# A post-norm decoder layer on one core: projections, feed-forward inputs and spline chunks dealt out in a new order

## The chip, the cores and the metric

The kernel runs on one core of a Trainium2 chip. The core has five engines that run their own instruction streams and meet at semaphores: TensorE (PE in the profile, with PEld for its weight loads), VectorE (DVE), ScalarE (ACT), GpSimd (POOL) and SyncE (SP). DMA transfers are issued from the streams of SP, ACT and POOL. TensorE writes its results to PSUM, from where VectorE and ScalarE copy them out.

The metric is the device time of one execution in microseconds. The kernel before took 601.08 us in the median of 3 runs (600.80, 601.08 and 601.48).

## The reference

The input is x, 8 sequences (batches) of 256 tokens with 512 features, and a context of the same shape, all in fp32. One layer is computed, with a layer norm after each of its three parts:

```
x = layernorm(x + attention(x))                   # 16 heads of 32, q, k, v through low-rank maps, softmax, Wo
x = layernorm(x + x * r)                          # r: per head r[t] = decay * r[t-1] + ctx[t] * ctx[t]
x = layernorm(x + down @ (silu(gate @ x) * up @ x))
```

The three feed-forward weights (512 x 2048, twice, and 2048 x 512) are not given: each is a cubic spline through about 8,000 control points, sampled at every weight. The kernel uses that a spline is a cubic between its knots, so it never builds the dense weights: per tile of 128 inner features it needs 64 numbers for each token (samples of x near the knots and moments of x over the pieces between them), and 64 x 128 spline samples as weights. These samples are made on the chip from control points ("taps").

## The kernel before, in words

**Tiling.** The 2048 tokens are four groups g of 512 tokens (GT, NG), and a group is two batches (bb). Heads are taken in quads of four. The attention loop has 4 groups x 2 batches x 4 quads = 32 steps, s0 to s31 (`steps`, L634). All engine calls go through `Ordered` (L299), which keeps program order on each engine, so every row of the profile carries line L308 and is known by its tile names.

**A step.** Step s first issues the score matmuls of step s + 1 (`scores`: 8 matmuls into four PSUM tiles sc of ps_big). Then it works on the exponentials of its own four heads: `transposed` (4 transposes a head into a PSUM tile tr_e), `evicted` (copy to eT: heads 0 and 2 by VectorE, 1 and 3 by ScalarE), in the order tr0, tr1, tr2, `fill(2)`, tr3, `fill(6)`; in group 3 the last is `fill(2)`. Between them stand the row maxima (nmax, VectorE) and exponentials (ScalarE) of step s + 1. Last comes `weighted`, 8 matmuls into av. An av tile serves two quads and is freed by a multiply with the reciprocal sums (rec) in the step after.

**PSUM.** Two pools of four tiles: ps_big holds sc, and ps_mm holds everything else of the loop: tr_e, the units' results, av, tr_r, tr_rec, tr_x2, ps_mom. A tile of ps_mm comes free when its eviction has read it.

**Units and fill.** `units` is a list of generators, each a piece of TensorE work cut into steps of one call: a projection (`project`: 4 matmuls of 128 x 512 for one of 4 rows of q, k or v of the next group, 12 units a group), an output (`output`: 4 matmuls with Wo for 128 tokens; its eviction adds x and starts a chain of norms), and the inputs of a feed-forward block (`inputs`: 8 pieces: four times 4 transposes of x2 with an eviction to x2T, then four times the matmuls of the moments ps_mom). `fill(n)` (L354) takes n pieces from the head of the list. After every second piece it runs `slot()`, which advances every chain of norms by a stage, and `some_taps()` (L442), which adds 0.62 to a counter and, for each whole, makes one chunk of spline samples: a load on SP into one of two tiles, and multiplies and adds on POOL into wg, wu or wd. Sixteen chunks are for gate and up, forty for down. Before each group's end the loop at L771 takes all remaining projections of the next group, and `load_x` puts the load of x of the group after next on SP; xT_g has one buffer.

**Chains.** A norm is `norm_plain` (a square with sum on ScalarE, then va and rs on POOL, then x on VectorE) and later `norm_wide` (its rc on VectorE waits for rs of POOL). Between them come the transposes tr_r of the recurrence r and the multiply h on VectorE that frees tr_r. `recur` loads and squares the context on POOL and scans it on VectorE.

**Inputs.** `inputs(b)` needs x2 of block b. Its eviction goes to a DRAM scratch (xd, md), and `windows` and `moments` read it back on SP into xg, of which two tiles exist. Inputs 0 and 1 are units of group 3.

**Feed-forward (L984 on).** For each block b of 512 tokens: 16 gate and up matmul pairs (`gate_up`), a gather of inter on SP, 64 thin matmuls y (`exact`), sums (`into_sums`, which end in DMAs fin<-sum from POOL) and `finish`, which adds the last matmuls into y. inputs(b + 1) is a unit of blocks 1 and 2; reads that were put off are issued after that block's gate_up.

Of the kernel before, what the change touches and what calls it, by code (L numbers as in the profile page):

```python
# [10 lines left out]
F32 = mybir.dt.float32  # L11
# [6 lines left out]
P = 128  # L18
# [297 lines left out]
def decoder_kernel(ctx: ExitStack, tc: tile.TileContext, x, xT, ctxT, wq, wkT, wvT, woT, wdownT, wup, decay, up_taps, down_taps, mom_f, sum_f, out, plan):  # L316
# [37 lines left out]
    def fill(n):  # L354

        for i in range(n):
            if units:
                next(units[0][1])
                units[0][2] -= 1
                if not units[0][2]:  # L360
                    units.pop(0)
            if i % 2:
                slot()
                some_taps()

# [52 lines left out]
    folded, qkvs, rs, sums, xs, yTs = {}, {}, {}, {}, {}, {}  # L418
    dram = ctx.enter_context(tc.tile_pool(name="dram", bufs=2, space=bass.MemoryType.DRAM))

    def taps():

        todo = [(up_taps, s, (wg, wu)) for s in range(INTER // 2 // CH)]
        todo += [(down_taps, s, (wd,)) for s in range(wd.shape[1] // CH)]
        loaded = []
        for at in range(len(todo) + 1):
            if at < len(todo):
                src, s, ws = todo[at]
                c = att.tile([P, 3, 4, CH], F32, tag="taps", name="taps", bufs=2)
                nc.sync.dma_start(out=c[:, : len(ws) + 1], in_=src[s])  # L430
                loaded.append(c)
            if at:
                _, s, ws = todo[at - 1]
                c = loaded.pop(0)
                for j, w in enumerate(ws):
                    c4 = c[:, j + 1]
                    nc.gpsimd.tensor_tensor(c4, c4, c[:, 0], ALU.mult)
                    nc.gpsimd.tensor_tensor(c4[:, 0:2, :], c4[:, 0:2, :], c4[:, 2:4, :], ALU.add)
                    nc.gpsimd.tensor_tensor(w[:, s * CH : (s + 1) * CH], c4[:, 0, :], c4[:, 1, :], ALU.add)
            yield  # L440

    def some_taps():  # L442
        made[0] += 0.62
        while made[0] >= 1:
            made[0] -= 1
            next(weights, None)

    weights, made = taps(), [0]
# [5 lines left out]
    def load_x(g):  # L454
        xT_g = early.tile([P, DC, GT], F32, tag="xT", name="xT_g")
        nc.sync.dma_start(out=xT_g, in_=xT[:, g * GT : (g + 1) * GT].rearrange("(c p) t -> p c t", p=P))
        return xT_g
# [10 lines left out]
    def project(g, name, m, xT_g):  # L468

        ps = ps_mm.tile([P, GT], F32, tag="mm", name=f"ps_{name}")  # L470
        for c in range(DC):
            if name == "v":
                lhsT, rhs = xT_g[:, c, m * P : (m + 1) * P], folded[name][:, c, :]
            else:
                lhsT, rhs = folded[name][:, c, m * P : (m + 1) * P], xT_g[:, c, :]
            nc.tensor.matmul(ps, lhsT=lhsT, rhs=rhs, start=(c == 0), stop=(c == DC - 1))
            if c < DC - 1:
                yield
        evict_qkv(g, name, m, ps)
        yield  # L480

    def projections(g, xT_g):
        qkvs[g] = group_tiles(g)
        return [[name, project(g, name, m, xT_g), DC] for name in "qkv" for m in range(DC)]
# [125 lines left out]
    w_v = early.tile([P, DC, D], F32, name="w_v")  # L610
    w_o = last.tile([P, DC, D], F32, name="w_o")
    folded.update(q=w_q, k=w_k, v=w_v)
    xT_g = early.tile([P, DC, GT], F32, tag="xT", name="xT_g")
# [42 lines left out]
    for name in "qv":  # L656
        for m in range(DC):
            for _ in project(0, name, m, xT_g):
                pass
    xT_g = load_x(1)  # L660
# [39 lines left out]
    def inputs(b):  # L700
# [5 lines left out]
        xg = pool.tile([P, NTILE // 2, GT], F32, tag="xg", name="xg", bufs=2)  # L706
        xgs[b] = xg
# [10 lines left out]
        if b > 1:  # L718
            reads.append(lambda: windows(xd, xt, xg))
        else:  # L720
            windows(xd, xt, xg)
        mo = ffn["mom"].tile([P, ND, GT], F32, tag="fin", name="mom")
        ps = {}
        for c in range(DC):
# [13 lines left out]
            if c == DC - 1:  # L738
# [4 lines left out]
                if b > 1:  # L743
                    reads.append(lambda: moments(md, xg))
                else:
                    moments(md, xg)
# [5 lines left out]
    for s, (g, bb, quad) in enumerate(steps):  # L752
        n = g * 2 + bb
        if quad == 0 and bb == 0:
            if g + 1 < NG:
                units += projections(g + 1, xT_g)
            else:
                first.close()
                open_inputs()
                units += [["i", inputs(0), 2 * DC], ["i", inputs(1), 2 * DC]]  # L760
        if quad == 0 and n:
            load_rows(n - 1)
            o = [["o", output(n - 1, qc), DC] for qc in range(2)]
            if bb and g + 1 < NG:
                units[1:1] = o[:1]
                units.append(o[1])
            else:
                units[1:1] = o
            chains.append(recur(n))
        more = s + 1 < len(steps)  # L770
        if more and steps[s + 1][0] != g:  # L771
            while any(u[0] != "o" for u in units):
                fill(4)
            if g + 2 < NG:
                xT_g = load_x(g + 2)
        if more:
            sc = scores(s + 1)
# [41 lines left out]
        fill(2)  # L819
# [7 lines left out]
        fill(6 if g + 1 < NG else 2)  # L827
# [18 lines left out]
    for _ in weights:  # L846
        pass
# [136 lines left out]
    for b in range(NG):  # L984
        if 0 < b < NG - 1:
            units.append(["i", inputs(b + 1), 2 * DC])
            fill(DC)
        for j in range(NTILE // 2):
# [5 lines left out]
            if b and j == 2:  # L994
                fill(DC)
# [75 lines left out]
```

## Time and profile before

| | |
|---|---|
| median of 3 runs | 601.08 us |
| span of the profiled execution | 599.9 us |
| time outside the span, against the median | 1.2 us |
| step 4 to 5, scores end to scores end (102.99 to 114.06) | 11.07 us |
| attention steps s24 to s31 (329.90 to 399.58) | 69.68 us, PE busy 63.46 |
| feed-forward (400 to 600) | PE busy 188.23 of 200 us |
| POOL busy, 60 to 146 us | 59.41 us |

In a row of the timeline the columns are the start, the length, the engine, the line and the operation with out<-in and its shape; a bracket gives the idle time of the engine just before it and what ended it. "x12" means that twelve equal instructions in a row are drawn together. A projection, output or moments row counts a matmul in two to four records, so `ps_k x4` is two pieces of a unit and takes about 1.8 us. A step is best measured from the end of its sc row to the end of the next.

### The profile page before, as it was taken

What the parts mean: (1) busy time and instruction counts of PE and PEld (TensorE: products, weight loads), DVE (VectorE), ACT (ScalarE), POOL (GpSimd) and SP (SyncE); (2) the same over time, 40 slices, a digit from 0 to 9 for tenths busy, and PEclk for the clock granted to TensorE, in tenths of its full rate; (3) what the DMA queues carried; (4) which work ended last, traced back from release to release, by engine and by line L of the source; (5) the groups of instructions that cost most, each with busy time, mean ns of one, the idle gap of its engine ahead of it and who ended that gap; (6) DMA issues with size and microseconds to landing.
All of it is one profiled execution on the core that took longest, in us unless ns stands there. A gap on an engine that the chain in (4) does not pass through costs nothing.

```text
span 599.9 us, 9721 instructions
## 1 busy us (share of the span) xinstructions
PE 573.7 (96%) x3327; PEld 289.1 (48%) x3327; DVE 335.5 (56%) x741; ACT 274.3 (46%) x820; POOL 229.3 (38%) x513
## 2 busy tenths in 40 slices
PE   8999999988899999999999899999999999999993
PEld 3544545545455555555555556444344434433432
DVE  0203645558686575786664877776826505714615
ACT  0114644655655645654554677564315314504412
POOL 0000496686554535365440212200361262242253
PEclk9999999999999999999999999999999999999997
DMA  8104134335334115323210564659219987985931
GB/s 289 71 0 153 34 122 144 105 98 174 94 85 158 50 59 176 107 89 124 70 54 2 174 155 109 170 154 213 47 72 248 195 232 179 226 216 135 216 128 70
DMA packets 41696, 77.95 MB, mean 130 GB/s; under 512 B 5952, under 2 KB 10448, under 8 KB 41648
## 3 DMA queue, kind: packets, MB, share of 16 engines
q1 hardware_dynamic: 34576, 62.75, 39.8%
q0 software_dynamic: 6064, 13.41, 6.8%
q10 hardware_dynamic: 1008, 1.18, 0.7%
q8 instruction: 26, 0.43, 0.3%
q14 instruction: 22, 0.18, 0.1%
HBM read 45.22 MB, written 11.12 MB: 94 GB/s over the span
## 4 chain that ended last, share of the span: by engine, by line
PE 77%; DVE 7%; DMA 6%; POOL 5%; issue 2%; ACT 2%; POOLq 0%; SPq 0%; DVEq 0%; ACTq 0%
PE y L308 10%; PE ps_q L308 8%; PE ps_k L308 8%; PE ps_v L308 8%; PE ps_o L308 6%; PE tr_e L308 6%; PE pg L308 5%; PE ps_s L308 5%; PE av L308 5%; PE pu L308 5%; PE sc L308 4%; POOL taps L308 3%; PE ps_mom L308 2%; DMA fin<-sum 2%; DVE nmax L308 2%
## 5 line engine op out<-in xcount | busy, mean ns | idle before, releaser
L308 ACT ACTIVATE e<-sc,nmax 128x256 f32<-128x256 f32 x256 | 120.0, 479 | 76.2 <-DVE nmax L308 76.0
L308 DVE TENSOR_REDUCE nmax<-sc 128x2 f32<-128x512 f32 x128 | 85.2, 682 | 72.0 <-PE sc L308 67.0
L308 POOL TENSOR_TENSOR taps<-taps 128x256 f32<-128x256 f32 (+1 forms) x144 | 87.9, 610 | 33.8 <-DMA taps<-in_down_taps 25.8
L308 PE MATMUL tr_e<-ident,e 128*128 128x128 f32 x512 | 68.0, 276 | 0.8 <-DVE h L308 0.7
L308 PEld LDWEIGHTS tr_e<-ident,e 128*128 128x128 f32 x512 | 57.3, 140 | 22.7 <-issue 19.1
L308 PE MATMUL y<-inter,wd 32*128 32x512 f32 x512 | 63.0, 598 | 0.0
L308 PE MATMUL ps_o<-w_o,yT 128*128 128x512 f32 x128 | 60.0, 600 | 0.3 <-ACT eT L308 0.3
L308 PE MATMUL ps_v<-w_v,xT_g 128*128 128x512 f32 x128 | 58.6, 598 | 0.9 <-DVE eT L308 0.9
L308 PE MATMUL ps_k<-xT_g,w_k 128*128 128x512 f32 x128 | 58.7, 600 | 0.5 <-DMA xT_g<-in_xT 0.5
L308 PE MATMUL ps_q<-xT_g,w_q 128*128 128x512 f32 x128 | 58.2, 596 | 0.9 <-DVE eT L308 0.9
L308 ACT ACTIVATION_READ_ACCUMULATOR e<-sc,nmax 128x1 f32 x256 | 53.1, 207 | 0.0
L308 DVE TENSOR_TENSOR inter<-pu,sg 128x512 f32<-128x512 f32 x64 | 41.2, 687 | 18.3 <-PE pu L308 9.4
L308 POOL TENSOR_TENSOR rs<-va,neghalf 128x1 f32<-128x1 f32 x48 | 28.9, 602 | 49.6 <-DVE va L308 46.9
L308 ACT ACTIVATE sg<-pg 128x512 f32<-128x512 f32 x64 | 37.3, 597 | 18.4 <-PE pg L308 18.4
L308 POOL TENSOR_SCALAR va<-ss 128x1 f32<-128x1 f32 x32 | 6.5, 203 | 100.7 <-ACT x L308 51.1
L308 DVE COPY eT<-tr_e 128x512 f32<-128x512 f32 x64 | 43.8, 684 | 0.8 <-PE tr_e L308 0.7
L308 PEld LDWEIGHTS y<-inter,wd 32*128 32x128 f32 x512 | 26.7, 184 | 32.7 <-issue 27.0
L308 PE MATMUL av<-eT,v_g 128*32 128x256 f32 x512 | 36.7, 385 | 5.0 <-ACT eT L308 2.7
L308 POOL TENSOR_TENSOR r<-r 128x1024 f32<-128x1024 f32 x8 | 15.2, 1895 | 66.0 <-DMA r<-in_ctxT 65.9
L308 ACT COPY eT<-tr_e 128x512 f32<-128x512 f32 x64 | 37.3, 583 | 2.4 <-PE tr_e L308 2.4
L308 PE MATMUL sc<-k_g,q_g 32*128 32x256 f32 x512 | 37.4, 401 | 0.2 <-ACT e L308 0.2
L308 PEld LDWEIGHTS ps_v<-w_v,xT_g 128*128 128x128 f32 x128 | 23.1, 190 | 26.0 <-issue 24.3
(106 smaller groups left out, 739.8 us busy)
## 6 DMA issues: line engine op xcount, KB each, us to landing
nat<-inter SPq DMA_DIRECT2D x64, 256.0 KB
taps<-in_down_taps SPq DMA_DIRECT2D x40, 256.0 KB
taps<-in_up_taps SPq DMA_DIRECT2D x16, 384.0 KB
xg<-xd SPq DMA_DIRECT2D x8, 616.0 KB
r<-in_ctxT SPq DMA_DIRECT2D x8, 512.0 KB
x_t<-in_x SPq DMA_DIRECT2D x16, 256.0 KB
fin<-sum POOLq DMA_DIRECT2D x16, 256.0 KB, 5.3
out<-h SPq DMA_DIRECT2D x16, 256.0 KB
```

What stands on the lines that cost most here:

```text
L308: return lambda *a, **k: self.tc.keep_in_program_order(f(*a, **k))
```

## The change

- `fill` takes a number of slots. Every step calls `fill(2, 1)` and then `fill(FILLS[g][quad % 2], 3)`: 7 and 6 pieces a step in turn in group 0, 8 and 8 in group 1, 7 and 8 in group 2, 6 and 6 in group 3, always with four slots. Before, it was 8, 8, 8 and 4 pieces, with as many slots as half of that.
- Projections follow ORDER: the first batch's v before the later q and k, and the second batch's v (v2, v3) last. The latter are projected within the group that uses them. `require` takes pieces from the list, without slots, until a named unit is done: q and k of a quad before its scores, v before `weighted`, and all but the last two units of group 3 before its start.
- Outputs and inputs are put at other places of the list. inputs(2) is a unit of group 3, no longer of block 1, and its reads are issued in block 0. xg is allocated at the first read (`gathered`).
- `some_taps` adds 0.5 for the first sixteen chunks and 0.66 after; chunks left at the start of group 3 are made there.
- `load_x` of a group is issued when v3 of the group before is projected, on ScalarE's queue for groups 2 and 3.
- xT_g and w_v move to the pool att, the taps tiles to early.
- After the loop the remaining units are taken with `fill(2)`.

```diff
--- before.py
+++ after.py
@@ -351,17 +351,23 @@
             if next(c, c) is c:
                 chains.remove(c)
 
-    def fill(n):
-
+    def fill(n, slots=None):
+
+        slots = n // 2 if slots is None else slots
         for i in range(n):
             if units:
                 next(units[0][1])
                 units[0][2] -= 1
                 if not units[0][2]:
                     units.pop(0)
-            if i % 2:
+            if (i + 1) * slots // n > i * slots // n:
                 slot()
                 some_taps()
+
+    def require(g, *names):
+
+        while any(u[0] == (g, name) for u in units for name in names):
+            fill(1, 0)
 
     def norm_plain(h, s, o, other=None):
 
@@ -415,7 +421,9 @@
 
 
 
-    folded, qkvs, rs, sums, xs, yTs = {}, {}, {}, {}, {}, {}
+    FILLS = (5, 4), (6, 6), (5, 6), (4, 4)
+    ORDER = [(name, int(m)) for name, m in ("q0", "k0", "v0", "v1", "q1", "k1", "q2", "k2", "q3", "k3", "v2", "v3")]
+    folded, qkvs, rs, sums, xs, yTs, xTs = {}, {}, {}, {}, {}, {}, {}
     dram = ctx.enter_context(tc.tile_pool(name="dram", bufs=2, space=bass.MemoryType.DRAM))
 
     def taps():
@@ -426,7 +434,7 @@
         for at in range(len(todo) + 1):
             if at < len(todo):
                 src, s, ws = todo[at]
-                c = att.tile([P, 3, 4, CH], F32, tag="taps", name="taps", bufs=2)
+                c = early.tile([P, 3, 4, CH], F32, tag="taps", name="taps", bufs=2)
                 nc.sync.dma_start(out=c[:, : len(ws) + 1], in_=src[s])
                 loaded.append(c)
             if at:
@@ -440,20 +448,21 @@
             yield
 
     def some_taps():
-        made[0] += 0.62
+        made[0] += 0.5 if made[1] < INTER // 2 // CH else 0.66
         while made[0] >= 1:
             made[0] -= 1
+            made[1] += 1
             next(weights, None)
 
-    weights, made = taps(), [0]
+    weights, made = taps(), [0, 0]
 
     def group_tiles(g):
         pool, tag = (att, "odd") if g % 2 else (early, "even")
         return [pool.tile([P, DC, GT], F32, tag=f"{n}_{tag}", name=f"{n}_g") for n in "qkv"]
 
     def load_x(g):
-        xT_g = early.tile([P, DC, GT], F32, tag="xT", name="xT_g")
-        nc.sync.dma_start(out=xT_g, in_=xT[:, g * GT : (g + 1) * GT].rearrange("(c p) t -> p c t", p=P))
+        xT_g = att.tile([P, DC, GT], F32, tag="xT", name="xT_g")
+        (nc.scalar if g > 1 else nc.sync).dma_start(out=xT_g, in_=xT[:, g * GT : (g + 1) * GT].rearrange("(c p) t -> p c t", p=P))
         return xT_g
 
     def evict_qkv(g, name, m, ps):
@@ -465,8 +474,9 @@
         else:
             nc.scalar.copy(o, ps)
 
-    def project(g, name, m, xT_g):
-
+    def project(g, name, m):
+
+        xT_g = xTs[g]
         ps = ps_mm.tile([P, GT], F32, tag="mm", name=f"ps_{name}")
         for c in range(DC):
             if name == "v":
@@ -477,11 +487,13 @@
             if c < DC - 1:
                 yield
         evict_qkv(g, name, m, ps)
-        yield
-
-    def projections(g, xT_g):
+        if g and (name, m) == ORDER[-1] and g + 1 < NG:
+            xTs[g + 1] = load_x(g + 1)
+        yield
+
+    def projections(g):
         qkvs[g] = group_tiles(g)
-        return [[name, project(g, name, m, xT_g), DC] for name in "qkv" for m in range(DC)]
+        return [[(g, f"{name}{m}"), project(g, name, m), DC] for name, m in ORDER]
 
     def recur(n):
 
@@ -607,10 +619,10 @@
     bd_vo = early.tile([P, P], F32, name="bd_vo")
     w_q = early.tile([P, DC, D], F32, name="w_q")
     w_k = early.tile([P, DC, D], F32, name="w_k")
-    w_v = early.tile([P, DC, D], F32, name="w_v")
+    w_v = att.tile([P, DC, D], F32, name="w_v")
     w_o = last.tile([P, DC, D], F32, name="w_o")
     folded.update(q=w_q, k=w_k, v=w_v)
-    xT_g = early.tile([P, DC, GT], F32, tag="xT", name="xT_g")
+    xT_g = xTs[0] = att.tile([P, DC, GT], F32, tag="xT", name="xT_g")
     for c in range(DC):
         nc.sync.dma_start(out=w_k[:, c, :], in_=wkT[c * P : (c + 1) * P, :])
         nc.scalar.dma_start(out=xT_g[:, c, :], in_=xT[c * P : (c + 1) * P, 0:GT])
@@ -655,9 +667,9 @@
         (nc.vector.tensor_copy if m % 2 else nc.scalar.copy)(w_q[:, m, :], ps)
     for name in "qv":
         for m in range(DC):
-            for _ in project(0, name, m, xT_g):
+            for _ in project(0, name, m):
                 pass
-    xT_g = load_x(1)
+    xTs[1] = load_x(1)
     chains.append(recur(0))
     sc = scores(0)
     es = [exponentials(0, j, sc[j]) for j in range(4)]
@@ -703,8 +715,12 @@
         xt = pool.tile([P, DC, GT], F32, tag="x2T", name="x2T")
         xd = dram.tile([4 * SPAN, GT], F32, tag="xd", name="xd")
         md = dram.tile([1, 20 * NTILE, GT], F32, tag="md", name="md")
-        xg = pool.tile([P, NTILE // 2, GT], F32, tag="xg", name="xg", bufs=2)
-        xgs[b] = xg
+
+        def gathered():
+            if b not in xgs:
+                xgs[b] = pool.tile([P, NTILE // 2, GT], F32, tag="xg", name="xg", bufs=2)
+            return xgs[b]
+
         for c in range(DC):
             tr = ps_mm.tile([P, GT], F32, tag="mm", name="tr_x2")
             for t in range(TC):
@@ -716,9 +732,9 @@
                 nc.sync.dma_start(out=xd[row : row + 4 * c - 3 : 4, :], in_=xt[:c, c, :])
             yield
         if b > 1:
-            reads.append(lambda: windows(xd, xt, xg))
+            reads.append(lambda: windows(xd, xt, gathered()))
         else:
-            windows(xd, xt, xg)
+            windows(xd, xt, gathered())
         mo = ffn["mom"].tile([P, ND, GT], F32, tag="fin", name="mom")
         ps = {}
         for c in range(DC):
@@ -741,9 +757,9 @@
                 nc.gpsimd.dma_start(out=md[:, : 2 * P].rearrange("h (c p) t -> (h p) c t", p=P), in_=mo[:, :2, :])
                 nc.gpsimd.dma_start(out=md[0, 2 * P :], in_=mo[:K2, 2, :])
                 if b > 1:
-                    reads.append(lambda: moments(md, xg))
+                    reads.append(lambda: moments(md, gathered()))
                 else:
-                    moments(md, xg)
+                    moments(md, gathered())
             yield
 
 
@@ -751,29 +767,31 @@
     pending = None
     for s, (g, bb, quad) in enumerate(steps):
         n = g * 2 + bb
-        if quad == 0 and bb == 0:
-            if g + 1 < NG:
-                units += projections(g + 1, xT_g)
-            else:
-                first.close()
-                open_inputs()
-                units += [["i", inputs(0), 2 * DC], ["i", inputs(1), 2 * DC]]
+        if quad == 0 and bb == 0 and g + 1 == NG:
+            require(g, *(f"{name}{m}" for name, m in ORDER[:-2]))
+            for _ in weights:
+                pass
+            first.close()
+            open_inputs()
         if quad == 0 and n:
             load_rows(n - 1)
             o = [["o", output(n - 1, qc), DC] for qc in range(2)]
-            if bb and g + 1 < NG:
-                units[1:1] = o[:1]
-                units.append(o[1])
+            i = [["i", inputs(b), 2 * DC] for b in range(3 if g + 1 == NG else 0)]
+            if bb == 0:
+                units += o[:1] + i[:1] + o[1:] + i[1:2]
+            elif g + 1 < NG:
+                at = 1 if units[0][2] > 1 else 2
+                units[at:at] = o[:1]
+                units[at + 2 : at + 2] = o[1:]
             else:
-                units[1:1] = o
+                units += o + i[2:]
             chains.append(recur(n))
+        if quad == 0 and bb == 0 and g + 1 < NG:
+            units += projections(g + 1)
         more = s + 1 < len(steps)
-        if more and steps[s + 1][0] != g:
-            while any(u[0] != "o" for u in units):
-                fill(4)
-            if g + 2 < NG:
-                xT_g = load_x(g + 2)
         if more:
+            g1, _, quad1 = steps[s + 1]
+            require(g1, f"q{quad1}", f"k{quad1}")
             sc = scores(s + 1)
         after = []
 
@@ -816,7 +834,7 @@
             nc.gpsimd.dma_start(out=y.rearrange("p q t -> p (q t)"), in_=from_)
         ahead(1)
         eTs.append(evicted(tr2, nc.vector.tensor_copy))
-        fill(2)
+        fill(2, 1)
         tr3 = transposed(es[3])
         ahead(2)
         if pending is not None:
@@ -824,7 +842,8 @@
             pending = None
         eTs.append(evicted(tr3, nc.scalar.copy))
         ahead(3)
-        fill(6 if g + 1 < NG else 2)
+        fill(FILLS[g][quad % 2], 3)
+        require(g, f"v{bb * 2}", f"v{bb * 2 + 1}")
         if quad % 2 and not short:
             tr = ps_mm.tile([P, 2, T], F32, tag="mm", name="tr_rec")
             for q in range(2):
@@ -843,8 +862,8 @@
         es = after
     nc.vector.tensor_tensor(pending[0], pending[1], pending[0], ALU.mult)
     nc.scalar.activation(neghalf[:, 3:4], neghalf[:, 2:3], AF.Silu)
-    for _ in weights:
-        pass
+    while units:
+        fill(2)
     mid.close()
     load_rows(NG * 2 - 1)
     units += [["o", output(NG * 2 - 1, qc), DC] for qc in range(2)]
@@ -982,7 +1001,7 @@
             slot()
 
     for b in range(NG):
-        if 0 < b < NG - 1:
+        if 1 < b < NG - 1:
             units.append(["i", inputs(b + 1), 2 * DC])
             fill(DC)
         for j in range(NTILE // 2):
@@ -991,7 +1010,7 @@
             gather(b, 2 * j + 1)
             if b:
                 slot()
-            if b and j == 2:
+            if b and j == 2 and units:
                 fill(DC)
         if b == 0:
             fill(2 * DC)
```

## The prediction

> **What bounds the kernel now.** I read the page's busy and clock rows, then the waits of PE (the list of what it waited for), then stretches of the trace by stage, then single stretches of the timeline.
>
> ```profile
> span 599.9 us, 9721 instructions
> PE 573.7 (96%) x3327; PEld 289.1 (48%) x3327; DVE 335.5 (56%) x741; ACT 274.3 (46%) x820; POOL 229.3 (38%) x513
> PEclk9999999999999999999999999999999999999997
> PE 77%; DVE 7%; DMA 6%; POOL 5%; issue 2%; ACT 2%; POOLq 0%; SPq 0%; DVEq 0%; ACTq 0%
> ```
>
> PE is busy 96% at full clock: only its 26 us of idle time, or time in which its order of work adds new waits, can move. By stage (columns: stretch, its length, busy time of PE, PEld, DVE, ACT, POOL, clock, DMA share, GB/s):
>
> ```profile
> 60.00:146.00 86.00, 82.83 (x505) 43.77 (x502) 48.55 (x93) 45.64 (x160) 59.41 (x114) 1.00 0.34 106
> 235.00:322.00 87.00, 86.14 (x514) 45.49 (x513) 58.25 (x136) 46.39 (x158) 41.06 (x74) 1.00 0.26 82
> 322.00:400.00 78.00, 71.78 (x538) 41.29 (x540) 59.52 (x137) 51.55 (x172) 15.71 (x25) 1.00 0.51 132
> 470.00:490.00 20.00, 20.00 (x152) 9.11 (x156) 6.63 (x18) 4.37 (x10) 8.80 (x28) 1.00 0.92 210
> ```
>
> Groups 0 and 3 (first and third line) leave PE 3.2 and 6.2 us; group 2 leaves 0.9; the start of the kernel has its own, untouched. Who ends the waits of group 0's end and group 1's start (110 to 185 us), and then of group 3 (322 to 400 us); columns: total, times, longest:
>
> ```profile
> PE av L308 <- DVE rec L308: 1.7, 1, 1.7
> PE av L308 <- ACT eT L308: 1.4, 1, 1.4
> PE ps_v L308 <- DVE eT L308: 0.9, 1, 0.9
> PE tr_e L308 <- DVE h L308: 0.7, 1, 0.7
> PE tr_r L308 <- ACT eT L308: 0.3, 1, 0.3
> ...
> PE av L308 <- DVE x2T L308: 2.3, 2, 1.2
> PE av L308 <- ACT eT L308: 1.3, 2, 1.0
> PE tr_rec L308 <- DVE mom L308: 0.8, 1, 0.8
> PE ps_mom L308 <- DVE mom L308: 0.8, 1, 0.8
> ```
>
> Nearly all are PSUM waits: PE wants one of the four buffers of ps_mm and an eviction is late. A regular step, in contrast, has none. Its timeline (start, length):
>
> ```profile
> 92.02 1.47 PE L308 MATMUL tr_e<-ident,e 128*128 128x128 f32 x12
> 93.41 1.98 PE L308 MATMUL ps_k<-xT_g,w_k 128*128 128x512 f32 x4
> ...
> 92.66 0.69 DVE L308 COPY eT<-tr_e 128x512 f32<-128x512 f32 x1
> ...
> 93.64 0.58 ACT L308 COPY eT<-tr_e 128x512 f32<-128x512 f32 x1
> ```
>
> The step's scores end at 91.91. Three transposed tiles go out back to back and end at about 93.4; the first eviction, eT0, lands at 93.35; then the first projection piece takes eT0's buffer at 93.41. So at a step's start av holds one buffer, tr0 to tr2 the other three, and the fill is released by eT0 exactly on time. Nothing is spare.
>
> **The change, part by part.** The matmuls are the same, so PE's work is the same.
>
> *a. Units that straddle steps.* Every unit of work (4 pieces; 8 for inputs) holds a ps_mm buffer from its first piece to its eviction. Before, 2+6 pieces a step end every unit inside its step. The new counts are 7 and 6 in group 0, 8 in group 1, 7 and 8 in group 2, 6 in group 3. Running sums modulo 4 give: group 0: 7, 13, 20, 26, 33, 39, 46, 52, so units stay open into s1, s2, s4, s5, s6, s7 (not s3, s8). Group 1: none. Group 2: 7, 15, 22, 30, 37, 45, 52, 60: open into s17 to s22. Group 3: 6, 12: into s25, then the inputs. In such a step the open unit holds a third buffer, so tr2 cannot go out with tr0 and tr1: it needs eT0's buffer, which lands 1.44 us after the step's start (93.35 - 91.91). Tr2's four transposes (0.437 of 12 in 1.31) then stand between that and the fill: 0.44 us a step. In s7 and s18 another tile (a recurrence transpose or a second unit) is open too: tr1 waits for eT0, and tr2 for ACT's eviction of tr1: 1.50 + 0.44 (tr1) + 0.64 (eviction 0.58 and its signal) + 0.44 (tr2) = 3.0 us after the start against 1.50 now: 1.5 us each. Sum: s1, s2, s4, s5, s6, s17, s19 to s22, s25 = 11 x 0.44 = 4.8, and 2 x 1.5 = 3.0: **+7.8**. The nearest rows of before are the 0.9 us of ps_v waiting for eT (above) and its twin of 0.85 at 263.53; nobody hides them. Ends: 0 (PE would have idled there anyway) and 13 x 0.9 = 11.7. I take 7.8, as the regular step shows the times to 0.05 us.
>
> *b. Chunks of taps.* Each slot advances the spline chunks on POOL by 0.62, four slots a step: 2.5 chunks; now 2 a step for the first 16, then 2.64. Up-chunks cost POOL 3.2 us. In before the norm chain stands behind one:
>
> ```profile
> 117.16 0.74 ACT L308 ACTIVATE x<-h,nm 128x512 f32<-128x512 f32 x1
> 121.83 1.25 POOL L308 TENSOR_TENSOR taps<-taps 128x256 f32<-128x256 f32 x2
> 123.57 0.18 POOL L308 TENSOR_SCALAR va<-ss 128x1 f32<-128x1 f32 x1
> ```
>
> ACT had its square sum at 118.0, POOL took it up at 123.57, the h that frees tr_r's buffer came late, and s6/s7 lost 0.7 + 0.9 + 0.3 + 1.4 = 3.2 us. I let that go whole: **-3.2** (ends -3.2 and +3.2: one more up-chunk in front of x1 in s7, since tr_r now meets an open unit). The 1.7 us at s9 is another case: a one-element multiply on DVE took 1.84 us beside POOL's 1.89 us square of r. Whether the new slots meet it is chance: **-0.9** (ends -1.7, 0). What is late next there is eT0, priced in a. The taps that are now behind stay on POOL and SP in groups 1 and 2, where POOL is busy 41 of 87 us; 57 chunks are done by group 3, so the new flush there costs nothing.
>
> *c. Second-batch v inside its group, required pieces.* The same 0.86 us a piece, moved; the wait of s18 in before (0.85) lies in the same place as the new one and is replaced: **-0.9**. The v pieces are asked for some steps before weighted() needs them.
>
> *d. Group 3: 6 pieces a step and a third inputs unit.* Steps s24, s25 get plain pieces instead of inputs and lose their waits of 0.3 + 1.2 + 0.8. Inputs 0, 1, 2 now lie in s26/27, s28/29, s30/31. Before, a step with four tr_x pieces ended in this:
>
> ```profile
> 335.31 0.68 DVE L308 COPY x2T<-tr_x 128x512 f32<-128x512 f32 x1
> 336.04 1.38 PE L308 MATMUL av<-eT,v_g 128*32 128x256 f32 x16 [1.16 <-DVE x2T L308]
> 337.11 0.60 ACT L308 COPY x2T<-tr_x 128x512 f32<-128x512 f32 x1
> ```
>
> With six pieces two moment pieces follow the four transposes, take two more buffers, and av's must come from the last x2T, ACT's, at 337.71: 7.8 us after that step's start (329.90), against 6.14 here. Step: 7.8 + 1.1 (av) + 1.1 (scores) = 10.0 to 10.7 (ACT also has a norm's square in front), against work of 7.9: +2.0 to 2.7 in s26 and s28 each; s27 and s29 by 1.35 (tr2 straddling 0.44 and the moments' wait of 0.8 as at 345.10), s30 0.3, s31 2.3 (like s28, without scores), FFN's first gate 1.0 (it waits for the moments' evictions). Sum 10.3 to 11.7. The same reckoning of before, step lengths over work at regular pace, is 9.8 (2.2, 1.0, 1.0, 0, 2.2, 2.4, 0.6, 0.4). **+0.5**, s25 counted in a; ends -6.2 (all its waits go) and +4. The 5.3 us of inputs(2) itself (16 transposes 1.75, moments 3.58) only moves from FFN to here.
>
> The Trainium skill has a rule for this part: "Perfetto Trace Analysis", Optimization Strategy, says that where the engine that binds changes from stage to stage, interleaving the stages may help. By it PE's surplus would fill group 3's gaps, d would be -6.2, and the sum 6.7 lower. The same page, Optimizing Tensor Performance, wants independent groups to rotate through PSUM banks so that an eviction overlaps the next group; the rows at 336.04 and 93.41 show that rotation already without a spare buffer.
>
> *e. FFN.* The third block's gathers on SP (2 MB) move from block 1, where DMA is at 0.92 of its engines, to block 0's stretch from 420 to 445 us, at 0.26. PE's wait at block 1's end (y <- DMA fin<-sum, 0.8 at 492.96) goes: **-0.8** (ends -2.0, both such waits; 0).
>
> *f. x by ScalarE.* Two loads of 1 MB leave SP and go to ACT behind v3's eviction, which waits for the same matmul, so nothing new is held on ACT but an issue of about 0.4 us, and ACT is busy 46%. **0**; lower end 0, as in before no projection in the loop waits for x. A load takes 6 to 7 us (issued 134.83, DMA busy to about 140), the need comes some 9 us after it; were it 2 us short twice, +4.
>
> Sum: 7.8 - 3.2 - 0.9 - 0.9 + 0.5 - 0.8 = +2.5. The profiled span is 599.9, the median 601.08, 1.2 more; so 601.08 + 2.5 = **603.6**.
>
> **Rivals.** *Gaps filled (faster).* The one question is the price of a straddle. If eT0 lands earlier than reckoned, or PE's slack in the step (0.3 us a regular step over its rows' work of 10.7) takes it up, a is 0 and the sum is -5.3: 595.8. It decides below 7.8 - 2.5 = 5.3 over 7.8, that is when a straddle costs less than two thirds of 0.44, 0.30 us. For it: PE already waits for eT0 there; against: DVE takes nmax first in program order (92.00 to 92.69).
> *A late chain (slower still).* x1 stands behind an up-chunk in s7 (+3.2 in place of nothing): 606.8, with x late on ACT up to 608 or so. For it: the rows at 121.83; against: 20% fewer chunks.
> *It cancels (same).* A straddle costs about 0.30, or group 3 gains 2.5: 601.1.
>
> **How the numbers follow.** This kernel's runs spread by 0.1%, so 0.2% (1.2 us) is about the least that tells from no change. Forecast, new PSUM waits outweigh the seam: 0.38; late chain: 0.14; together slower 0.52. Gaps filled: 0.35. Cancels: 0.13. The range reaches from the faster rival's 595.8 to the late chain's 608; beyond that lie a's upper end (+3.9) and d's lower end. The likeliest case alone spans 602.3 to 606.
>
> **What would show it.** Right: in s1, s2, s4 to s6 and s17 to s22 twelve transposes no longer lie together: eight, then four after a wait of about 0.4 us for eT, step lengths 0.44 over their pieces; s7 and s18 with the longest waits; av in s26 and s28 waiting for ACT's x2T; no va late on POOL in s6; no y wait at block 1. Wrong: a free PE row between tr1 and tr2, or group 3's idle well under 5 us; ps_k or ps_q waiting for xT_g.

## The result and the profile after

The changed kernel takes 615.7 us in the median of 4 runs (615.47 to 615.94), the kernel before 601.28 us beside it. The ratio is 1.0239, with a 95% interval of 1.0224 to 1.0253: 14.4 us slower. The sign was forecast, the size (2.5 us) and the range (up to 608.0) were not.

From the page of the changed kernel:

```profile
span 613.6 us, 9729 instructions
PE 578.2 (94%) x3327; PEld 292.0 (48%) x3327; DVE 334.7 (55%) x741; ACT 274.3 (45%) x820; POOL 231.7 (38%) x513
PEclk9999999999999999999999989799999999999997
PE 77%; DVE 9%; issue 5%; DMA 4%; POOL 2%; ACT 2%; POOLq 0%; DVEq 0%; ACTq 0%; SPq 0%
```

PE has as many instructions as before, but is busy 4.5 us longer, and two slices of its clock row read 8 and 7. The change adds no PE work, so the same work ran slower there. Idle time rose from 26 to 35 us.

To see where, I cut both traces at the starts of s0, s8, s16, s24 and at the first gate, and took from each stretch the pieces of units in it (0.86 us for a projection or output piece, 0.44 for four transposes of x2, r or the sums, 0.89 for a moments piece), since the change moves pieces between stretches. Here and below a step runs from its first transposes to those of the next step. What is left must be equal if only pieces moved:

| stretch | before: length, less pieces | after: length, less pieces | difference |
|---|---|---|---|
| group 0 | 87.02, 37.55 | 84.91, 38.88 | +1.3 |
| group 1 | 92.17, 35.39 | 91.19, 33.97 | -1.4 |
| group 2 | 91.79, 34.57 | 92.05, 38.27 | +3.7 |
| group 3 | 69.68, 42.23 | 89.99, 49.90 | +7.7 |
| feed-forward | 200.32, 181.06 | 196.76, 183.69 | +2.6 |

The sum is 13.9, less 0.2 us at the start of the kernel: the 13.7 us between the spans. Over half lies in group 3, which the prediction had at +0.5. What PE waited for in the changed kernel (total, times, longest):

```profile
PE tr_e L308 <- DVE eT L308: 10.7, 15, 1.9
PE tr_e L308 <- DVE mom L308: 2.6, 2, 1.3
PE y L308 <- DMA fin<-sum: 2.3, 2, 1.5
PE ps_o L308 <- DVE eT L308: 1.7, 1, 1.7
PE tr_e L308 <- ACT eT L308: 1.5, 2, 0.7
```

Before, tr_e waited 0.9 us in all. In most straddling steps the wait looks like s2 here:

```profile
78.44 1.09 PE L308 MATMUL tr_e<-ident,e 128*128 128x128 f32 x8
79.93 0.66 PE L308 MATMUL tr_e<-ident,e 128*128 128x128 f32 x4 [0.39 <-DVE eT L308]
80.42 1.88 PE L308 MATMUL ps_v<-w_v,xT_g 128*128 128x512 f32 x4
```

Eight transposes, 0.39 us of waiting, then the third tile, and only then the fill: the form that the prediction gave in part a.

Group 3 is something else. Around the start of s27 (timeline of ScalarE, GpSimd and VectorE, then PE):

```profile
350.34 0.74 ACT L308 ACTIVATE x<-h,nm 128x512 f32<-128x512 f32 x1
353.33 0.62 ACT L308 COPY x2T<-tr_x 128x512 f32<-128x512 f32 x1
354.24 1.07 POOL L308 DMA_DIRECT2D xd<-x2T  x2 [2.30 <-ACT x2T L308]
355.39 0.18 POOL L308 TENSOR_SCALAR va<-ss 128x1 f32<-128x1 f32 x1
356.25 0.55 DVE L308 TENSOR_SCALAR x<-h,nm,rs 128x512 f32<-128x512 f32 x1 [4.34 <-POOL rs L308]
356.71 0.68 DVE L308 COPY mom<-ps_mom 128x512 f32<-128x512 f32 x1
357.45 1.26 PE L308 MATMUL tr_e<-ident,e 128*128 128x128 f32 x8 [1.30 <-DVE mom L308]
...
360.66 1.11 PE L308 MATMUL tr_e<-ident,e 128*128 128x128 f32 x4 [1.95 <-DVE eT L308]
361.70 3.10 PE L308 MATMUL ps_mom<-x2T,mf 128*64 128x512 f32 x8
364.73 0.66 PE L308 MATMUL tr_e<-ident,e 128*128 128x128 f32 x4
```

The norm's sum of squares was there at 351.2. POOL took it up at 355.39, because two DMA issues stood in front that waited for ScalarE's x2T copy. VectorE, in order, stood 4.34 us at the x that needs it, and behind x waited the moments' copy, h, and the row maxima. PE lost 1.30 and 1.95 us. Then it ran slow: eight moments records in 3.10 us, against 1.97 in the kernel before. The stretches show why (columns as in the prediction):

```profile
356.00:358.00 2.00, 0.70 (x8) 0.42 (x4) 1.75 (x4) 0.00 (x0) 0.21 (x1) 1.00 0.56 173
358.00:360.00 2.00, 0.71 (x5) 0.42 (x4) 1.93 (x7) 0.00 (x0) 0.00 (x0) 1.00 0.10 39
360.00:362.00 2.00, 1.34 (x6) 1.01 (x8) 1.39 (x4) 1.96 (x8) 0.00 (x0) 0.67 0.61 179
362.00:364.00 2.00, 2.00 (x6) 0.47 (x4) 0.50 (x1) 0.46 (x2) 0.00 (x0) 0.50 0.75 142
364.00:366.00 2.00, 1.81 (x9) 0.72 (x6) 1.09 (x5) 0.58 (x1) 0.17 (x1) 0.98 0.75 154
```

After 4 us in which PE was busy 1.4, the granted clock fell to 0.50 for 3.4 us. The same happens in s29 for 6.8 us (384.6 to 391.4). Steps s26 to s29 take 11.2, 14.3, 11.2 and 14.9 us.

The feed-forward stage, parts d and e: the wait of block 1 for fin<-sum is gone, but block 0 now has one of 1.54 us at 464.80 (before: none there). Its stretch now carries the third block's reads; with them back in block 1 (run 2) block 0 has no such wait. The first gates wait 1.25 us for ScalarE's silu to free a buffer. Together with block 2's wait, now 0.7 instead of 1.24, that is 1.5 of the 2.6 us; the rest I have not located.

### The profile page after: what moved, and what is told of

The parts are those of the page before. It is cut to its first block, busy times and chain, and to the rows that moved or that the text cites. A ratio compares the mean times of both kernels' runs of the same rounds, so it can differ in the third digit from the quotient of the medians.

```text
span 613.6 us, 9729 instructions
## 1 busy us (share of the span) xinstructions
PE 578.2 (94%) x3327; PEld 292.0 (48%) x3327; DVE 334.7 (55%) x741; ACT 274.3 (45%) x820; POOL 231.7 (38%) x513
## 4 chain that ended last, share of the span: by engine, by line
PE 77%; DVE 9%; issue 5%; DMA 4%; POOL 2%; ACT 2%; POOLq 0%; DVEq 0%; ACTq 0%; SPq 0%
PE y L308 10%; PE ps_k L308 9%; PE ps_q L308 8%; PE ps_v L308 8%; PE ps_o L308 8%; PE tr_e L308 7%; PE ps_s L308 5%; PE pg L308 4%; PE pu L308 4%; PE sc L308 4%; PE av L308 4%; DMA fin<-sum 2%; DVE nmax L308 2%; DVE eT L308 2%; DMA md<-mom 1%
## 5 line engine op out<-in xcount | busy, mean ns | idle before, releaser
L308 POOL TENSOR_TENSOR taps<-taps 128x256 f32<-128x256 f32 (+1 forms) x144 | 90.2, 626 | 16.7 <-DMA taps<-in_down_taps 10.9
L308 PE MATMUL tr_e<-ident,e 128*128 128x128 f32 x512 | 73.0, 280 | 14.8 <-DVE eT L308 10.7
L308 PE MATMUL ps_k<-xT_g,w_k 128*128 128x512 f32 x128 | 60.1, 598 | 0.5 <-DVE eT L308 0.5
L308 PE MATMUL pg<-xg,wg 64*128 64x512 f32 x128 | 37.5, 599 | 1.3 <-ACT sg L308 1.3
L308 PE MATMUL pu<-xg,wu 64*128 64x512 f32 x128 | 36.8, 589 | 0.0
```

The source lines that it names most:

```text
L308: return lambda *a, **k: self.tc.keep_in_program_order(f(*a, **k))
```

## The experiments

My theory after the result: two causes, PSUM straddles in groups 0 and 2, and in group 3 a queue (norm steps on POOL behind DMA issues) whose gaps also cost PE its clock. The rivals: PSUM alone explains group 3; the third inputs unit overloads it; the order of units or the x load is to blame.

**1. The writes to DRAM on SyncE.**

```diff
-            nc.gpsimd.dma_start(out=xd[c : ...
+            nc.sync.dma_start(out=xd[c : ...
-                nc.gpsimd.dma_start(out=md[...], in_=mo[...])     # both of them
+                nc.sync.dma_start(out=md[...], in_=mo[...])
```

> The changed kernel with the DRAM writes of the inputs (xd from x2T, md from mom) issued by SyncE instead of GpSimd. Theory POOL-queue: in group 3 the first norm's va and rs stand on POOL behind these DMA issues, which wait for ScalarE's x2T copy; VectorE, in order, holds x, the moments' copy and the row maxima behind them. Then the waits of 1.30 and 1.95 us at the start of s27 and s29 go, the granted clock stays at 1.00 there, and the time falls by 6 to 10 us, to 606 to 610 us. Theory PSUM-only: the four buffers of ps_mm are too few whatever POOL does; the same waits stay and the time stays within 2 us of 615.7 us.

Measured: 644.7 us, ratio 1.0697 (1.0647 to 1.0747). The waits named did go: s26 and s27 took 10.21 and 10.89 us instead of 11.16 and 14.28. But the total missed by far, as SyncE became the queue. Its timeline, and what PE then waited for:

```profile
380.94 1.70 SPq L308 DMA_DIRECT2D xg<-md  x2
382.67 0.96 SPq L308 DMA_DIRECT2D x_t<-in_x  x2
383.75 7.86 SPq L308 DMA_DIRECT2D xd<-x2T  x3
391.66 2.06 SPq L308 DMA_DIRECT2D r<-in_ctxT  x1
...
381.73 1.93 PE L308 MATMUL av<-eT,v_g 128*32 128x256 f32 x16 [6.67 <-DVE mom L308]
408.32 1.91 PE L308 MATMUL av<-eT,v_g 128*32 128x256 f32 x10 [13.32 <-ACT eT L308]
```

SyncE holds the reads that wait for a write's round trip through DRAM (xg<-md), and behind them the second unit's writes (8 us later than in the changed kernel, 375.63) and the last batch's context r (13.5 us later, 378.14). So half of the theory is supported for s26 and s27, and the edit is no clean test of the total.

**2. The third inputs unit back in block 1.**

```diff
-            i = [... for b in range(3 if g + 1 == NG else 0)]
+            i = [... for b in range(2 if g + 1 == NG else 0)]
-        if 1 < b < NG - 1:
+        if 0 < b < NG - 1:
```

> The changed kernel with the third block's inputs made in block 1 of the feed-forward stage again; all else as changed. Theory POOL-queue and PSUM alike: inputs 0 and 1 still stall s27 and s29, so only the costs that belong to the third unit go: the wait of 1.25 us of the first gates for the moments' copies, 0.3 us at s31 and 0.7 us of fin<-sum in block 0, about 2 us; 613 to 614 us. Rival (the third unit is what overloads group 3): 8 us or more go, 605 to 608 us.

Measured: 616.2 us, ratio 1.0230 (1.0189 to 1.0271). Moving the third unit is neutral, as the 5.3 us were expected to be; the small gains named were not seen either (fin<-sum fell to 1.3 us in all, but the first gates still waited 1.2 us, for the copy of yT). The rival of an overload by this unit falls. s27 and s29 stay at 14.26 and 14.86.

**3. Aligned counts.**

```diff
-    FILLS = (5, 4), (6, 6), (5, 6), (4, 4)
+    FILLS = (6, 6), (6, 6), (6, 6), (2, 2)
```

> The changed kernel with 8 pieces a step in groups 0 to 2 and 4 in group 3 (as before the change), so that every projection and output unit ends inside its step. Second-batch v is then projected a group ahead again, and the rest of the third inputs unit comes after the loop. Theory straddle: the waits of tr_e for eT in groups 0 to 2 (6.5 us and more in the changed kernel) go, group 3 falls back to its 10 us over its work, the clock stays up, and the pace of the chunks keeps its gain at s6 and s7: 597 to 601 us. Rival (the order of the units or the x load costs it): no more than half comes back, 608 us or more.

Measured: 618.3 us, ratio 1.0261 (1.0220 to 1.0302), 17 us above what was expected. The waits of tr_e in groups 0 to 2 went, except 0.5 at s7, but other waits took their place:

```profile
143.36 1.05 PE L308 MATMUL av<-eT,v_g 128*32 128x256 f32 x10 [1.81 <-ACT eT L308]
148.66 1.98 PE L308 MATMUL ps_o<-w_o,yT 128*128 128x512 f32 x4 [1.72 <-DVE eT L308]
```

These are s7 and s8; s15 and s23 wait 1.44 us each for VectorE's eT, as s8 does. In front of that eviction VectorE has steps of a norm (at s8 x at 146.64, eT at 147.93). From s0 to s24 this run takes 275.5 us and the kernel before 271.0, for the same 184 pieces and although the new pace of the chunks is in it. The changed kernel does eight pieces (6.9 us) fewer and begins s24 only 3.1 us earlier, so it is 3.8 us behind. Aligned counts did not bring groups 0 to 2 back, and the rival is not out there. No run separates what in the order of units does it.

A single step prices the straddle. Where s2 takes 11.18 us with eight aligned pieces, seven would take 10.32; the changed kernel takes 10.72: 0.40 us. Group 3 was slow again, with only four pieces and three slots a step:

```profile
379.32 0.54 POOL L308 DMA_DIRECT2D xd<-x2T  x1 [2.34 <-ACT x2T L308]
379.94 0.18 POOL L308 TENSOR_SCALAR va<-ss 128x1 f32<-128x1 f32 x1
380.81 0.55 DVE L308 TENSOR_SCALAR x<-h,nm,rs 128x512 f32<-128x512 f32 x1 [3.82 <-POOL rs L308]
381.55 2.15 DVE L308 COPY wide<-rec 128x512 f32<-128x512 f32 x1
384.95 1.12 PE L308 MATMUL tr_e<-ident,e 128*128 128x128 f32 x4 [4.12 <-DVE eT L308]
```

It is the same queue at another step, s29. The wait goes when these issues stand behind va (run 7).

**4. PE kept busy in the gaps.** This kernel computes the next step's scores twice in s27 and s29 and the transposes of the second head five times, into the same tiles; the added matmuls are redundant.

```diff
             sc = scores(s + 1)
+            if s in (27, 29):
+                scores(s + 1, sc)
...
-        tr1 = transposed(es[1])
+        tr1 = transposed(es[1], 5 if s in (27, 29) else 1)
```

> The changed kernel with redundant PE work in the idle stretches of s27 and s29: the scores of the next step are computed twice (1.1 us) and the transposes of the second head five times (1.75 us more), into the same tiles. Theory clock: the half clock in s27 and s29 follows from PE's idle time there; with the gaps filled the clock stays at 1.00, the rows after them return to their length (8 moments matmuls in 2.0 us instead of 3.1 to 3.7), and in spite of 5.7 us more PE work the time falls by about 4 us, to 611 to 613 us. Rival: the clock has another cause, or the added work delays VectorE: the time stays or rises, 615 to 620 us.

Measured: 613.9 us, ratio 1.0191 (1.0146 to 1.0236). The interval touches that of the changed kernel, so the total alone decides nothing; the trace does. The two steps took 12.65 and 12.66 us instead of 14.28 and 14.87, with 5.7 us more work in them, and the clock is full in the stretches that read 0.67 and 0.50:

```profile
360.00:362.00 2.00, 1.80 (x12) 0.91 (x12) 1.56 (x3) 2.00 (x9) 0.00 (x0) 1.00 0.41 135
362.00:364.00 2.00, 1.80 (x9) 0.72 (x6) 1.05 (x5) 0.70 (x3) 0.13 (x1) 1.00 0.76 145
...
360.91 1.94 PE L308 MATMUL ps_mom<-x2T,mf 128*64 128x512 f32 x8
```

So the half clock follows from PE's idle time there and costs 3.8 us in the two steps. The medians differ by only 1.8 us; in this trace the clock also fell to 0.50 in s31 (398 to 401 us), where the changed kernel's stayed full.

**5. Two DMA issues behind the norm.** x2T's third and fourth part go to xd at the start of the next piece, so va and rs come first on POOL.

```diff
-            nc.gpsimd.dma_start(out=xd[c : ...
+            if c < 2:
+                nc.gpsimd.dma_start(out=xd[c : ...
...
             yield
+        for c in range(2, DC):
+            nc.gpsimd.dma_start(out=xd[c : ...
         if b > 1:
             reads.append(lambda: windows(...
```

> The changed kernel with one reordering on GpSimd: the DMA issues of x2T's third and fourth part to xd come one piece later, behind the norm's va and rs instead of in front of them. Theory POOL-queue: VectorE's x no longer waits 4.3 us in s26 and s28; s26 with s27 fall from 25.4 to about 21.1 us as with the writes on SyncE (10.21 and 10.89), s28 with s29 likewise, no half clock, 606 to 608 us. Rival PSUM-only: s27 and s29 keep their waits, 614 us or more.

Measured: 611.7 us, ratio 1.0166 (1.0148 to 1.0184). s26, s27 and s28 take 10.21, 10.89 and 10.23 us, as expected of the queue; PSUM alone had these waits stay. The total is 4 us short of the expectation since s29 takes 15.68:

```profile
374.95 0.39 SPq L308 DMA_DIRECT2D r<-in_ctxT  x1
385.91 1.89 POOL L308 TENSOR_TENSOR r<-r 128x1024 f32<-128x1024 f32 x1 [9.11 <-DMA r<-in_ctxT]
387.83 0.69 DVE L308 TENSOR_TENSOR_SCAN r<-dec,r 128x256 f32<-128x256 f32 x1 [4.62 <-POOL r L308]
390.69 1.05 PE L308 MATMUL av<-eT,v_g 128*32 128x256 f32 x10 [3.36 <-ACT eT L308]
```

A new wait takes the old one's place: the last batch's context lands 11 us after its issue, and the scan that needs it stands on VectorE in front of the row maxima. The clock fell once more after this wait (0.50 from 392 to 394 us).

**6. The pace alone, in the kernel before.**

```diff
-        made[0] += 0.62
+        made[0] += 0.5 if made[1] < INTER // 2 // CH else 0.66
```

> The kernel before with the changed pace of the chunks alone (0.5 a slot for the first sixteen, then 0.66). Prediction's part b: the waits at s6 and s7 (3.2 us) go and half of that at s9: 597 to 599 us. Rival (the seam waits come from the order of units, which is as before here): within 1 us of the kernel before.

Measured: 599.1 us, ratio 0.9960 (0.9945 to 0.9975): 2.4 us less than the kernel before. On POOL, the norm no longer stands behind a chunk (va at 117.65, right after its sum). What is left of the five waits between 110 and 185 us:

```profile
PE av L308 <- ACT eT L308: 1.4, 1, 1.4
PE av L308 <- DVE rec L308: 1.0, 1, 1.0
PE tr_r L308 <- ACT eT L308: 0.3, 1, 0.3
```

s6 falls from 12.88 to 11.02 us. The 1.4 us of s7 stay, so that one was not POOL's; of s9's 1.7 us, 1.0 stays.

**7. Both, aligned counts and the two DMA issues behind the norm.** The edits of 3 and 5 together.

> The changed kernel with both: 8 pieces a step in groups 0 to 2 and 4 in group 3, and the two DMA issues behind va and rs. If the straddles and the POOL queue are the two causes, groups 0 to 2 keep the 2.7 us that they gained on the kernel before with 8 pieces, and group 3 loses its wait of 4.1 us at s29 and the half clock: 606 to 610 us. Rival (group 3 with this order of outputs and inputs is bound elsewhere): within 2 us of 618.3 us.

Measured: 612.2 us, ratio 1.0177 (1.0160 to 1.0194), 2 us above what was expected. s29 falls from 16.18 to 11.26 us, so the queue was its cause. Half of what is left stands in groups 0 to 2, which take 5.5 us more than in the kernel before for the same pieces; the expectation had counted on a gain of 2.7 us there, which run 3 does not show. Group 3 is still slow at s25 and s26 (9.16 and 11.28 us), with waits for the evictions of eT and x2T.

**8. The kernel before with the pace and the two DMA issues.** The edits of 5 and 6 on the kernel before.

> The kernel before with the changed pace and with the two DMA issues one piece later. Against the run with the pace alone this prices the POOL queue in the kernel before, where va stood behind those issues once (s28): 0 to 2 us less than the pace alone, 596 to 598 us. If the DMA issues hold nothing there, the two are equal.

Measured: 598.9 us, ratio 0.9957 (0.9942 to 0.9972): equal to the pace alone. In the kernel before the issues hold nothing; the queue is a cost of the new order only.

**9. The last context load from ScalarE.** As 5, and:

```diff
-        nc.sync.dma_start(out=r, in_=ctxT[...])
+        (nc.scalar if n == 7 else nc.sync).dma_start(out=r, in_=ctxT[...])
```

> The changed kernel with the two DMA issues behind va and rs, and with the last batch's context load (r) issued by ScalarE instead of SyncE. In the run without the latter, the load stood on SyncE behind the reads of the first block's moments, landed late, and the scan on VectorE held the row maxima of s29 (scores there waited 3.4 us for eT, step 15.7 us against 10.9 of s27). Theory: a queue again, not PSUM: s29 falls to about 11 us, 606 to 608 us. Rival: DMA bandwidth is short there (share 1.0), the load lands late from any queue, and the time stays at 611 to 612 us.

Measured: 611.9 us, ratio 1.0182 (1.0150 to 1.0214): no gain. The issue came only 0.9 us earlier (374.06), after the transposes that still read the buffer (373.37), and POOL could use the data at 385.34, 11 us later again. s29 fell to 13.28 us, but s28 rose to 11.23. My queue explanation of the late load falls. What is left is that the issue waits for the buffer and that the DMA engines are busy (a share of 1.08 from 378 to 382 us); neither was tested by itself.

**10. The open unit first.** As 9, and in a step that begins inside a unit, one piece of it goes out before tr2.

```diff
+        going = 1 if units and units[0][2] % DC else 0
+        fill(going, 0)
         tr2 = transposed(es[2])
...
-        fill(2, 1)
+        fill(2 - going, 1)
```

> As the run with r on ScalarE, and in steps that begin inside a unit one piece of that unit goes out before the third transposed tile. The piece needs no new buffer, so it covers the wait for eT. Theory straddle: the waits of 0.35 to 0.39 us in ten steps go, and about 0.9 each of those at s7 and s18: 4 to 6 us less than the run with r on ScalarE, 601 to 603 us. Rival: the wait is only pushed to the next buffer (the second piece's unit or tr3), and less than 2 us is gained.

Measured: 605.6 us, ratio 1.0073 (1.0058 to 1.0089), 6.3 us less than run 9 beside it. s2 now reads:

```profile
78.01 1.09 PE L308 MATMUL tr_e<-ident,e 128*128 128x128 f32 x8
78.94 1.02 PE L308 MATMUL ps_v<-w_v,xT_g 128*128 128x512 f32 x2
79.80 0.60 PE L308 MATMUL tr_e<-ident,e 128*128 128x128 f32 x4
```

No wait, and the step takes 10.10 us instead of 10.72. One piece of a unit that already has its buffer covers the wait for eT, which is the prediction's mechanism shown by removing it. By the traces, 5.2 of the 6.3 us lie in groups 0 and 2 and at s25, where the straddles are. s7 and s18 still wait (1.64 us, and 0.78 and 0.69).

**11. The context's chain four slots later.** As 10, and:

```diff
+        for _ in range(4 if n == 7 else 0):
+            yield
         nc.gpsimd.tensor_tensor(r, r, r, ALU.mult)
```

> As the run in which the open unit goes first, with the square and scans of the last batch's context put four slots later, so that its load (some 10 us on busy DMA engines) has landed when VectorE comes to the scan. Theory: with four slots a step in group 3 instead of two, chains come due in half the time, and the scan that waits for the load is what still holds s29; its wait of 2.7 us goes and the step falls from 13.9 to about 10.6 us: 601.5 to 603.5 us. Rival (s29 is held by something else, or the scan's wait is as long later): 605 us or more.

Measured: 602.9 us, ratio 1.0016 (0.9998 to 1.0034). s26 to s29 take 10.20, 10.62, 11.25 and 10.62 us, and the clock is full throughout group 3. With the causes found so far removed, the change is level with the kernel before, though not with run 6.

**12. And the third unit in block 1 again.** The edits of 11 and 2.

> As the run with the r chain later, and with the third block's inputs in block 1 of the feed-forward stage again. If the third unit in group 3 has a cost of its own that the other stalls hid (1.8 us before a piece of s30, 1.3 us at the first gates, 1.5 us of block 0's fin<-sum), 2 to 3 us less than that run; if moving it is neutral, as with the stalls in place, equal within 1 us.

Measured: 602.5 us, ratio 1.0013 (0.9999 to 1.0027), equal to run 11. Moving the third inputs unit is neutral in both settings.

## Why the prediction was wrong

**Right: a, straddles.** The steps named show the form named. Ten of the eleven single ones wait 0.35 to 0.41 us, s6 0.58, against 0.44; s7 and s18 waited 1.84 + 0.73 and 0.78 + 0.73 us, against 1.5 each. The waits add up to 8.3 us against 7.8, and removing the single ones gave up to 6.3 (run 10 against 9). That the sum came so close is partly luck: the single ones were smaller, and s7 was larger for a reason that b has wrong. The faster rival needed less than 0.30 us a straddle, so it is out. Run 3 adds a caution: without straddles groups 0 to 2 were no faster, as other waits came in.

**Right in kind, a little large: b, the pace.** -3.2 and -0.9 at s6, s7 and s9 measured as -2.4 us in all (run 6). The step that failed is "I let that go whole": 1.4 us of s7 wait for something else. In the changed kernel s7 begins with VectorE's x waiting 2.74 us for POOL's rs behind an up-chunk (va at 129.25), so part of the late-chain rival came true there.

**As said: c.** PE's old wait at s18, 0.85 us for a buffer of ps_q, is gone and tr_e waits there instead. No run tests c alone.

**Wrong: d, group 3,** and this is where the result left the range. The part was put at +0.5 us, the lower end of its own sum (10.3 to 11.7 less 9.8), and measured +7.7. "s27 and s29 by 1.35" was the failing term (its two parts, 0.44 and 0.8, also add up to only 1.24); they took 14.3 and 14.9 us, against 10.6 once the causes were removed. I had reckoned buffers only. Left out were:
- the POOL queue: the xd issues wait for ScalarE, and the norm's va behind them now holds VectorE. In the kernel before, the same issues waited 2.44 us on POOL at s24 and s28, and at s28 va stood behind them too, with no harm (run 8), so the row was there, without its price; I asked who waits for av, not what stands behind the issue on POOL. These rows are from s28 of the kernel before:

```profile
372.50 1.06 POOL L308 DMA_DIRECT2D xd<-x2T  x2 [2.44 <-ACT x2T L308]
373.64 0.18 POOL L308 TENSOR_SCALAR va<-ss 128x1 f32<-128x1 f32 x1
373.91 0.56 POOL L308 TENSOR_TENSOR rs<-va,neghalf 128x1 f32<-128x1 f32 x1
377.60 0.54 DVE L308 TENSOR_SCALAR x<-h,nm,rs 128x512 f32<-128x512 f32 x1
```

- the pace of slots: four slots a step instead of two bring each chain's next stage due in half the time. In the rows above VectorE came to x 3.1 us after rs was there; in the changed kernel it stood idle at x for 4.34 us until rs came. The same pace brought the scan ahead of its load, and putting the scan four slots later removed that wait (run 11). That the pace also moved x is read from the traces, not tested.
- the clock: gaps were priced at their length. The kernel before showed a full clock with gaps of up to 1.74 us, and I took it to hold. 3.8 us come from this (run 4).

Run 5 gives 4 us for the first, clock included, with the second already eating into it; run 11 takes 2.8 us less than run 10, with the scan's wait removed.

By the Trainium skill's rule on interleaving ("Perfetto Trace Analysis", Optimization Strategy), as part d reads it, group 3 would have gained 6.2 us. With the queue, the straddles and the scan out of the way (run 11), its length less pieces is 41.5 us against 42.2 before: a gain of 0.7. The stages can be interleaved, but PE's gaps there were not free capacity: in run 11 PE still waits there for the evictions of mom and eT.

**Wrong in place: e.** Block 1's wait went as said; block 0 got one of 1.54 us instead. I looked at the DMA share where the reads went (0.26) and not at whose transfer comes next there. In run 2 the reads are back in block 1, and the wait is in block 1 again (0.71 us).

**Not contradicted: f.** The changed kernel shows no wait for xT_g in the loop. No run tests it alone. Group 1 gained 1.4 us (s9's wait went).

About 1 us of the feed-forward stage's loss stays unexplained. Run 11, which has the pace's gain of 2.4 us in it, is still not faster than the kernel before. By its trace the feed-forward stage loses 2.8 us and group 2 loses 1.6. In s7 PE still waits 2.07 us, as VectorE's x waits 2.75 us for POOL's rs behind an up-chunk (va at 127.52), and in this execution the clock then stood at 0.50 from 131.6 to 135.0 us. No run removed that wait, so what it costs is not shown.

## What to carry to other kernels

A work list dealt out in pieces can put a piece of the open unit in front of the next claim on a buffer. That gained 6.3 us here, while ending the units at those points (run 3) brought other waits. Before a step is made denser, list for every in-order queue, DMA issues included, what stands behind each instruction that waits; and count slots, not only work, since chains advance by slot. A gap on the matmul engine in a stage that already has gaps is to be priced above its length.

## What the runs showed of the hardware

In the changed kernel PE's granted clock stood at 0.50 for 3.4 us in s27 and for 6.8 us in s29. In the 3.4 us before the fall PE was busy 1.27 and 1.73 us, with no single gap above 1.95 us. After it PE worked without a break in s27, and in s29 for all but the first 1.6 us. In run 11 it was busy 1.34 of the 3.4 us before the fall at 131.6 us. The Trainium skill, "TensorE: Matmul & The Clock Gate", What's actually happening, puts the fall to half at an idle window of about 3.4 us; here 3.4 us that were about 40% busy were enough. A fixed share does not come out of these traces: 1.66 us of work in the 3.4 us from 398.2 in the changed kernel, and 1.76 in the 3.4 us from 155.3 in the kernel before, left the clock at 1.00.

A VectorE instruction of one element per partition took 1.84 us, and a copy of 128 x 512 took 2.15 us instead of 0.43, each while POOL squared r (1.89 us in the kernel before, 1.91 in run 3).
